# Cross-attention with layer norm: another order of all engines' work from the third tile on

## The chip, the cores and the metric

The kernel runs on one core of one Trainium2 chip. The metric is the device time of one execution in microseconds (us), the median over the runs. The engines are TensorE (PE in the profile, PEld for its weight loads), VectorE (DVE), ScalarE (ACT), GpSimd (POOL) and SyncE (SP), which issues most DMAs.

## The reference

```python
qs = (q @ wq).reshape(Bq, Lq, H, HD).transpose(0, 2, 1, 3)      # q is x: (4, 2048, 512); 16 heads of 32
ks_ = (k @ wk).reshape(Bq, Lk, H, HD).transpose(0, 2, 1, 3)     # k and v are the context: (4, 77, 512)
vs = (v @ wv).reshape(Bq, Lk, H, HD).transpose(0, 2, 1, 3)
scores = jnp.einsum('bhqd,bhkd->bhqk', qs, ks_) / jnp.sqrt(jnp.float32(HD))
scores = jnp.where(mask[:, None, :, :], -jnp.inf, scores)
attn_w = jax.nn.softmax(scores, axis=-1)
attn = jnp.einsum('bhqk,bhkd->bhqd', attn_w, vs)
out = attn.transpose(0, 2, 1, 3).reshape(Bq, Lq, H * HD) @ wo + q
mu = jnp.mean(out, axis=-1, keepdims=True)
var = jnp.mean((out - mu) ** 2, axis=-1, keepdims=True)
return (out - mu) / jnp.sqrt(var + EPS) * gamma + beta
```

All in float32. The kernel keeps the precision of the two projections with three products of a high and a low part of each operand (hi x hi, hi x lo, lo x hi).

## The kernel before, in words

The 8192 rows of x are 64 tiles of 128 rows; two tiles make a block (0 to 31) and four a group. Keys and values are made once at the start. Then every tile goes through the same steps, and the steps of many tiles are interleaved. **The order is written out by hand**, in a table of words, `ORDER` (lines 49 to 142): a letter for the step, a number for the tile, block or group, and sometimes a part. The loop at lines 732 to 744 reads it word by word and issues each step's instructions; each engine then runs its own instructions strictly in that order. The words that matter here:

- `Q` (line 275, TensorE): one quarter of a group's queries, 12 matmuls; `q` (289, VectorE) copies it out of its bank. `g`, `i`, `j` load the group's transposed x (262, SyncE), make its high part (265, ScalarE) and its low part (269, GpSimd).
- `S` (405, TensorE): the scores of a tile, 64 small matmuls into four banks. `T` (422, VectorE): mask and row maxima, four heads per word, one bank each; four words make a tile. `e` (437, ScalarE): four exponentials with their sums. `r` (447, VectorE): reciprocals of the sums; `n` (452, GpSimd): normalise; `t` (473, VectorE): transpose into B, one B per block.
- `P` (484): one of the twelve DMAs by which a block's B becomes PT, issued by the engine of its last letter: `s` SyncE, `a` ScalarE, `g` GpSimd. The words with `a` and `g` begin with block 23 and block 25.
- `V` (498, TensorE): the block's 32 matmuls with the values, into two banks; `a` (527, ScalarE) and `b` (531, VectorE): their high and low parts AH and AL.
- `O` (554, TensorE): the output product of a tile, 12 matmuls in one bank; `+` (563, VectorE) adds x, which `x` (539, SyncE) loads; `s` (577, 578, VectorE) and `v` (583 to 586, GpSimd) are the statistics; `k` (592, ScalarE), `f` (595, GpSimd) and `)` (598, GpSimd) are scale, gain and shift; `w` (601, SyncE) stores the tile. The last eight tiles use other steps for the norm.

`SLOTS` (lines 146 to 171) gives each tile buffer its place, in the order in which the table asks for them; `mm` are the eight PSUM banks. A step that takes a bank waits until the bank's last reader is done. Three buffers `pbuf` hold a tile between its maxima and its transpose, so that `T` of a tile waits for `t` of the tile three earlier.

The layer below gives each DMA of SyncE and ScalarE one of eight completion semaphores (DMAHW0 to DMAHW7), and GpSimd's one of eight others. A DMA waits, on the engine that issues it, until the DMA that had its semaphore before has landed.

Of the kernel before, what the change touches and what calls it, by code (L numbers as in the profile page):

```python
# [54 lines left out]
P1.9s P1.1s q9 Z1.s P1.11s r4 Q10 q10 e6.2 e6.1 j6 e6.3 D1 S5 T5.1 T5.3 e5.3 D2 T5.0 e5.0 Q8 q8 e6.0 j7 n4 t4 Z0.s
e5.1 S7 T7.3 e7.3 r6 T7.1 e7.1 P1.3s g8 Z5.s Z4.s T5.2 e5.2 T7.2 n6 Q14 q14 Q11 q11 Z16.s x4 g9 L1 Z13.s e7.2 Q13
Z15.s T7.0 t6 S9 T9.3 T9.0 e7.0 r7 n7 V1 T9.1 a1.0 b1.0 T9.2 r5 e9.3 x3 a1.1 b1.1 t7 P3.10s P3.1s x0 P3.11s P3.5s V0
a0.0 e9.2 b0.0 P3.6s i9 n5 t5 P2.5s O2 P3.3s P3.8s P3.9s e9.0 e9.1 S8 a0.1 T8.0 e8.0 T8.1 T8.2 e8.2 e8.1 b0.1 +2 T8.3
s2 P2.0s r9 O3 +3 s3 i8 P3.0s P3.2s O0 e8.3 j9 P3.7s P3.4s S10 T10.3 +0 T10.2 T10.0 q13 v1 k3 e10.3 r8 e10.0 T10.1
P2.2s g11 P2.11s n9 Z8.s Z14.s P2.9s P2.7s P2.6s e10.1 k2 O1 +1 s0 s1 P2.10s Q15 q15 n8 t8 Q12 P2.4s q12 S11 T11.1  # L60
T11.0 T11.2 =16.8 e10.2 v0 i11 =24.8 T11.3 r10 V3 a3.1 t9 P2.3s a3.0 b3.0 x6 P2.1s S12 T12.1 P2.8s b3.1 T12.2 x7 f2 j8
Q18 e11.0 e11.2 k1 n10 P4.4s g10 O7 f3 q18 P4.11s P4.10s )3 w3 j11 P4.9s g12 P4.5s )2 P4.6s P4.2s T12.0 S13 P4.3s V2
P4.0s T12.3 t10 e12.1 +7 s7 e11.3 e12.2 e11.1 r11 O6 T13.0 f1 P4.8s a2.1 n11 P4.7s b2.1 e12.0 P4.1s T13.2 T13.1 t11
P5.7s P5.4s +6 s6 v3 Z6.s P5.1s w2 x8 P5.10s i10 e13.0 a2.0 e12.3 e13.1 e13.2 Q19 q19 P5.3s S14 T14.3 T14.2 P5.6s r12
# [5 lines left out]
O8 +8 s8 v4 T18.2 T18.3 T18.1 e17.3 e17.0 Q20 b5.0 x10 e18.3 r17 T18.0 e18.0 e18.2 q20 n16 t16 Q21 S19 T19.0 T19.3  # L70
T19.2 T19.1 q21 P7.0s P7.2s P7.3s k8 k5 a5.1 g14 j13 x11 Q23 Z10.s q23 x13 g15 n17 f5 e18.1 r18 e19.2 Q25 t17 q25 )5
k9 V6 b5.1 S20 a6.0 e19.1 b6.0 a6.1 e19.3 e19.0 O10 n18 t18 T20.2 f9 +10 b6.1 T20.1 T20.3 )9 O11 f8 P8.3s i14 j14 L2
P8.1s S21 T21.3 w5 )8 +11 T21.1 r19 n19 Z7.s P8.0s P8.10s P8.7s P8.5s w9 T21.0 s11 T20.0 P8.2s x12 P8.9s V7 k4 e20.3
T21.2 i15 j15 O13 t19 s10 S22 T22.2 +13 e20.2 a7.0 e21.0 e20.1 e20.0 r20 e21.2 v5 f4 n20 g16 b7.0 s13 P8.8s P8.11s
e22.2 O12 +12 P8.6s T22.3 P8.4s )4 Q27 a7.1 b7.1 T22.1 t20 P9.0s P9.5s q27 P9.6s P9.10s Z12.s w8 T22.0 s12 v6 P9.8s
Q24 q24 g17 e22.3 e21.1 e21.3 r21 n21 P9.3s x16 P9.4s Q26 q26 S23 T23.2 T23.1 T23.3 k10 f10 P9.11s P9.7s e22.1 e22.0
r22 )10 n22 P9.2s k13 e23.3 T23.0 t21 V8 a8.0 S24 T24.3 Q29 P9.1s e23.0 a8.1 e23.2 T24.0 e23.1 i16 T24.2 f13 )13 b8.0
b8.1 j16 O14 P9.9s t22 T24.1 x14 +14 s14 P10.7s P10.9s P10.4s k12 e24.0 e24.1 r23 S25 T25.1 T25.3 T25.2 T25.0 e24.3
i17 e25.1 e24.2 n23 O15 x15 +15 s15 k11 w4 O16 P10.5s v7 P10.8s P10.2s t23 S26 e25.0 T26.1 j17 T26.2 P10.0s x17 w13
P10.6s +16 T26.0 f11 P10.10s r24 P10.3s k14 n24 V9 a9.1 k15 f15 T26.3 e26.3 a9.0 e25.2 e25.3 e26.1 g18 P10.11s P10.1s  # L80
w10 P11.4s P11.11s x18 O17 +17 s17 P11.1s P11.2s q29 s16 t24 r25 Q28 q28 b9.0 b9.1 Q31 q31 Q30 q30 P11.10s S27 T27.2
P11.9s P11.6s P11.0s P11.5s f14 v8 x19 P11.7s P11.8s n25 )14 e26.2 e26.0 k16 r26 e27.2 n26 T27.0 T27.1 k17 f16 )16 V10
a10.0 e27.1 a10.1 f17 )15 T27.3 e27.3 t25 S28 P11.3s g19 T28.3 T28.2 b10.1 t26 T28.1 P12.0s P12.5s O19 P12.9s P12.2s
P12.6s e28.3 O18 +18 s18 w16 +19 b10.0 Q33 q33 w14 )17 )11 w15 e27.0 r27 T28.0 n27 i19 j19 i18 e28.1 S29 T29.1 e29.1
P12.7s e28.0 V11 T29.3 T29.0 P12.10s P12.11s x21 x20 P12.1s t27 P13.5s P13.10s P12.4s g20 O21 P12.8s P13.8s O20 a11.0
T29.2 b11.0 s19 P13.2s v9 =32.8 a11.1 b11.1 e28.2 r28 n28 j18 e29.0 k18 f18 )18 S30 T30.1 e30.1 +20 T30.0 e30.0 k19
f19 T30.3 s20 +21 s21 v10 T30.2 P13.9s P12.3s x23 P13.7s P13.6s w18 P13.3s P13.0s P13.11s P13.4s w17 Q35 q35 e30.3
e29.2 P13.1s =40.8 e29.3 t28 w11 r29 n29 Q32 q32 S31 T31.2 T31.1 T31.3 O23 T31.0 e30.2 r30 n30 e31.1 Q34 q34 V12 e31.3
a12.0 t29 P14.5s L3 P14.7s f12 k21 f21 P14.2s x22 S32 T32.3 i20 g21 T32.2 b12.0 P14.9s a12.1 P14.1s P14.10s x24 )19
# [5 lines left out]
e36.2 r34 T36.1 +27 b14.1 T36.3 P16.0s O26 n34 t34 x29 f23 f22 )23 e35.2 k24 f24 P16.1s S37 T37.3 T37.2 T37.1 w12
e36.1 e35.3 T36.0 r35 n35 x28 P16.8s P16.9s w23 Q43 )24 )22 +26 P16.6s e36.3 P16.5s e37.1 a14.0 P16.3s P16.10s P16.2s
P16.4s P16.7s s27 x31 T37.0 P16.11s b14.0 Q40 V15 q40 s26 t35 P17.8s P17.2s e36.0 e37.3 v13 i22 q43 j22 P17.7s P17.3s
P17.10s P17.1s a15.0 b15.0 r36 n36 e37.2 k25 a15.1 e37.0 f25 S38 T38.2 e38.2 P17.11s )25 k26 P17.0s T38.1 O28 k27
T38.0 b15.1 +28 e38.1 r37 T38.3 e38.0 s28 Q42 q42 P17.9s w22 g24 P17.5s O29 +29 s29 w24 t36 Q41 q41 e38.3 S39 T39.1
e39.1 T39.3 e39.3 r38 T39.0 V16 a16.1 n37 t37 T39.2 S40 T40.2 T40.0 T40.1 v14 f26 k28 P17.4s P17.6s g25 T40.3 O31  # L100
b16.1 +31 e39.0 x32 s31 x30 a16.0 b16.0 P18.2s P18.1s P18.8s n38 t38 k29 e39.2 r39 O30 +30 S41 T41.2 T41.1 s30 f28 )28
Q47 q47 w28 P18.5s P18.4s Q45 P18.7s T41.3 T41.0 f27 i24 x33 )26 j24 n39 v15 t39 P18.3s e40.3 e40.2 e40.1 i25 f29 )27
w25 e41.2 e41.1 e41.0 P18.10s S42 T42.3 T42.1 T42.0 V17 k31 e40.0 T42.2 )29 a17.1 r40 n40 b17.1 k30 e41.3 e42.2
P18.11s q45 P18.0s O32 +32 P18.9s P18.6s O33 =48.8 +33 s33 a17.0 S43 e42.1 V18 a18.1 a18.0 e42.3 t40 r41 s32 g27
P19.0s P19.1s T43.3 T43.2 w27 f31 j25 n41 T43.0 T43.1 x35 P19.3s P19.5s e43.0 Q46 P19.10s w29 q46 f30 v16 P19.4s
P19.8s w26 P19.7s t41 P19.2s x34 b17.0 e42.0 r42 n42 e43.3 )30 Q44 q44 Q50 g26 P19.6s P19.9s x39 S44 T44.3 P19.11s )31
i27 j27 b18.0 T44.1 T44.2 q50 e43.2 e43.1 r43 n43 P20.6s Q48 b18.1 P20.1s t42 w31 P20.2s e44.1 i26 j26 k33 f33 )33 k32
e44.3 S45 T45.1 q48 T45.0 e45.0 T44.0 O34 O35 P20.10s +34 s34 T45.2 t43 P20.5s =56.8 Q51 V19 f32 P20.0s x36 P20.4s +35
# [692 lines left out]
```

## Time and profile before

| | us |
|---|---|
| median of three runs | 510.7 (510.17 to 511.24) |
| the profiled execution's own time | 511.24 |
| its span, first to last instruction | 509.4 |
| busy: PE, DVE, ACT, POOL | 500.0, 460.0, 474.0, 420.9 |
| mean granted TensorE clock | 0.996 |

A page shows one execution on the chip. Times in the timeline are from the span's start. An instruction counts as busy while it runs; matmuls are pipelined and their ends are modelled, so that short waits of TensorE can hide in its busy time. Where an engine was idle, the row has the time in brackets, and the last releaser that the profile finds. SPq, ACTq and POOLq are the engines' queues, where DMAs are issued; an issue is no busy time.

### The profile page before, as it was taken

To read this page: it belongs to the slowest core of one execution; us is meant where nothing else is said; L and a number is where in the kernel's file an instruction comes from. 1 tells how busy PE (TensorE), PEld (TensorE's weight loads), DVE (VectorE), ACT (ScalarE), POOL (GpSimd) and SP (SyncE) were. 2 spreads that over 40 slices of the span, in tenths; PEclk is the share of its full clock that TensorE was granted. 3 is DMA by queue.
4 is the path that set the end of the run, shared out by engine and by line. 5 is a ranking of instruction groups with operands and counts; after the bars stand their busy time and mean duration, and the time that the engine had idled before them with its cause. 6 is when DMAs were issued, how large, how long until landed. Compare 5 with 4: busy or idle time off the path is not lost.

```text
span 509.4 us, 20326 instructions
## 1 busy us (share of the span) xinstructions
PE 500.0 (98%) x6831; PEld 383.1 (75%) x6831; DVE 460.0 (90%) x2539; ACT 474.0 (93%) x2248; POOL 420.9 (83%) x387
## 2 busy tenths in 40 slices
PE   8999999999999999999999999999999999999995
PEld 6987778777777777777777777777787677867773
DVE  5799989988999998988998998899898989899997
ACT  6699999999999999999999999999997999899851
POOL 3665655978899789978898988899997999989995
PEclk9999999999999999999999999999999999999998
DMA  8957757889788978577986897868679659887745
GB/s 305 396 215 175 164 157 203 215 212 241 185 264 243 230 190 230 157 205 187 252 241 206 199 246 234 236 167 237 196 206 262 190 171 260 231 210 215 189 156 226
DMA packets 58782, 110.86 MB, mean 218 GB/s; under 512 B 9462, under 2 KB 11278, under 8 KB 58678
## 3 DMA queue, kind: packets, MB, share of 16 engines
q1 hardware_dynamic: 54502, 101.30, 70.7%
q0 software_dynamic: 2496, 5.77, 4.2%
q10 hardware_dynamic: 1680, 2.49, 1.8%
q8 instruction: 54, 0.88, 0.8%
q14 instruction: 50, 0.41, 0.3%
HBM read 41.79 MB, written 16.78 MB: 115 GB/s over the span
## 4 chain that ended last, share of the span: by engine, by line
PE 80%; DMA 5%; DVE 5%; SPq 4%; ACT 2%; POOL 2%; issue 1%; ACTq 0%; DVEq 0%; POOLq 0%
PE pq L275 29%; PE po L554 29%; PE pa L498 9%; PE sc L405 9%; DMA out<-o 2%; SPq L484 2%; DMA PT<-B 2%; DVE B L473 2%; PE pv L326 2%; PE pk L299 1%; ACT pbuf L437 1%; SPq L539 1%; DVE pbuf L422 1%; PE pq L685 1%; DMA xtf<-xT 1%
## 5 line engine op out<-in xcount | busy, mean ns | idle before, releaser
L437 ACT ACTIVATE pbuf<-pbuf,nm 128x77 f32<-128x77 f32 x1024 | 352.9, 353 | 8.4 <-DVE q L289 3.4
L437 ACT ACTIVATION_READ_ACCUMULATOR pbuf<-pbuf,nm 128x1 f32 x1024 | 197.9, 193 | 0.0
L422 DVE CUSTOM_DVE_ANT_0 pbuf<-sc,mb 128x77 f32<-128x77 f32 x1024 | 170.4, 232 | 13.4 <-PE sc L405 11.2
L452 POOL TENSOR_TENSOR pbuf<-pbuf,ri 128x1232 f32<-128x1232 f32 x63 | 142.0, 2258 | 34.6 <-DVE ri L447 28.2
L554 PE MATMUL po<-woh,AH 128*128 128x512 f32 x256 | 104.6, 409 | 0.2 <-DVE AL L531 0.2
L275 PE MATMUL pq<-xth,wqh 128*128 128x512 f32 (+1 forms) x256 | 99.9, 390 | 0.2
L554 PE MATMUL po<-woh,AL 128*128 128x512 f32 x256 | 100.0, 391 | 0.0
L554 PE MATMUL po<-wol,AH 128*128 128x512 f32 x256 | 100.0, 390 | 0.0
L473 DVE STREAM_TRANSPOSE B<-pbuf 128x1280 f32<-128x1280 f32 x64 | 95.8, 1500 | 3.4 <-DMA out<-o 0.9
L275 PE MATMUL pq<-xtl,wqh 128*128 128x512 f32 (+1 forms) x256 | 98.1, 383 | 0.0
L275 PE MATMUL pq<-xth,wql 128*128 128x512 f32 (+1 forms) x256 | 98.1, 383 | 0.0
L422 DVE DVE_READ_ACCUMULATOR2_ANT nm<- 128x1 f32 x1024 | 84.6, 83 | 0.0
L595 POOL TENSOR_TENSOR o<-o,gam 128x512 f32<-128x512 f32 x56 | 72.1, 1292 | 3.9 <-ACT o L592 3.8
L598 POOL TENSOR_TENSOR o<-o,bet 128x512 f32<-128x512 f32 x56 | 71.9, 1291 | 1.6
L269 POOL TENSOR_TENSOR xtl<-xtf,xth 128x1024 fp32r<-128x1024 f32 x28 | 67.2, 2401 | 4.8 <-ACT xth L265 4.0
L405 PEld LDWEIGHTS sc<-kct,q 32*64 32x64 f32 x4096 | 51.9, 130 | 24.9 <-issue 12.6
L405 PE MATMUL sc<-kct,q 32*64 32x77 f32 x4096 | 62.2, 238 | 1.5 <-DVE nm L422 0.9
L554 PEld LDWEIGHTS po<-woh,AH 128*128 128x128 f32 x256 | 48.0, 187 | 16.4 <-issue 3.5
L498 PE MATMUL pa<-PT,vsb 96*32 96x256 f32 x992 | 59.7, 382 | 0.0
L275 PEld LDWEIGHTS pq<-xth,wqh 128*128 128x128 f32 x256 | 48.1, 188 | 11.4 <-issue 0.8
L554 PEld LDWEIGHTS po<-woh,AL 128*128 128x128 f32 x256 | 48.1, 188 | 10.9 <-DVE AL L531 0.4
L275 PEld LDWEIGHTS pq<-xth,wql 128*128 128x128 f32 x256 | 48.1, 188 | 9.6
(108 smaller groups left out, 638.2 us busy)
## 6 DMA issues: line engine op xcount, KB each, us to landing
PT<-B SPq DMA_DIRECT2D x330, 128.0 KB
xtf<-xT SPq DMA_DIRECT2D x28, 512.0 KB
o<-x SPq DMA_DIRECT2D x56, 256.0 KB
out<-o SPq DMA_DIRECT2D x56, 256.0 KB
PT<-B POOLq DMA_DIRECT2D x25, 128.0 KB, 4.7
PT<-B ACTq DMA_DIRECT2D x17, 128.0 KB
stage_a<-kin SPq DMA_DIRECT2D x4, 410.0 KB
xtf<-xT SPq DMA_DIRECT2D x4, 256.0 KB
```

The lines of the kernel that those rows point to most:

```text
L269: return nc.gpsimd.tensor_tensor(l[:, c : c + 2], fx.pop((g, c)), xh[g][:, c : c + 2].bitcast(F32), ALU.subtract)
L275: nc.tensor.matmul(pq, w[:, c, m * P : (m + 1) * P], r[g][:, c, rs], start=(n == 0), stop=(n == 11))
L326: nc.tensor.matmul(pv[: rows.stop - rows.start], ctx_s[c][i][:, rows], v[c], start=(n == 0), stop=(n == 11))
L405: mm = nc.tensor.matmul(sc[j][r0 : r0 + SR, g * NK : (g + 1) * NK], qs[q, g, rs.start + r0 : rs.start + r0 + SR], kct[q, g, t // TPB, keys ...
L422: nc.vector.tensor_tensor_reduce(pb[:, h // 2, (h % 2) * NK : (h % 2 + 1) * NK], scs[t][j][:, g * NK : (g + 1) * NK], mb[:, t % TPB, keys_ ...
L437: nc.scalar.activation(pb[:, h // 2, (h % 2) * NK : (h % 2 + 1) * NK], pb[:, h // 2, (h % 2) * NK : (h % 2 + 1) * NK], AF.Exp, bias=nmax[t ...
L452: return nc.gpsimd.tensor_tensor(pv, pv, rv.to_broadcast((P, NP, 2, NK)), ALU.mult)
L473: nc.vector.transpose(bt.rearrange("p c q r -> p q c r"), pbuf[t % NPB].rearrange("p q (c r) -> p q c r", c=5),)
L498: nc.tensor.matmul(pas[b, g // 2][HD * j : HD * (j + 1), (g % 2) * BLK : (g % 2 + 1) * BLK], vsb[:, 2 * b // TPB, h % 2, HD * (h // 2) : H ...
L554: nc.tensor.matmul(pos[t], a[:, c, rs], w[:, c, :], start=(first and c == 0 and n == 0), stop=(c == NC_D - 1 and n == 2),)
L595: return nc.gpsimd.tensor_tensor(od[t], od[t], gam, ALU.mult)
L598: return nc.gpsimd.tensor_tensor(od[t], od[t], bet, ALU.add)
```

## The change

The table `ORDER` holds the same 2,138 words in another order; the first 60 are the same, up to the first words of the third tile. `SLOTS` follows, since buffers are asked for in another order. No step, mask or statistic is changed, and each word stays on its engine. TensorE's row is nearly the same sequence of visits: now and then a `Q` and an `O`, or an `S` and a `V`, change places. Cut to four lines of the table, and the places:

```diff
 ORDER = """
...
-e14.1 S16 T16.2 e14.3 r14 a4.1 b4.1 O9 T16.1 T15.3 P6.3s T16.0 P6.1s T16.3 e15.0 n14 t14 w7 e15.1 P6.9s S17 P6.5s
...
-e52.2 P24.8s V23 a23.0 n51 q59 t51 w40 P24.0s P24.4s P24.6s S53 O45 a23.1 )41 w41 v21 w38 e52.0 k42 P25.7a e52.3 T53.0
...
+i13 e15.3 e16.3 e16.1 P6.8s r15 n15 e16.2 S17 T17.2 g14 P6.6s V5 a5.0 a5.1 e17.2 T17.1 T17.0 T17.3 x9 P6.5s s4 t15
...
++42 w39 P24.4s S53 T53.0 s42 v21 T53.3 e53.0 P24.3a x44 i30 V23 a23.0 j30 P24.5s t51 P25.6s P25.4s w35 P24.8s T53.2
...
 SLOTS = {
     "mm": (
-        "5012367450123456702315467023616312047536420762403712056301425672015467154206701253467021534062571347"
...
+        "5012367450123456702315467023614372546310642574032165070153462705627345064723517024635120462314507614"
...
-    "xtf": "010101100101010101101010101010",
+    "xtf": "010101010101010110101010101010",
-    "o": "765401234567146204172036574036751430267521403657143201756423057",
+    "o": "765401234567215640520163527645132045173620154730264705316407215",
-    "nm": "0120120120120120120120120120120120120120120120120120120120120120",
+    "nm": "0120120121021021021021021021021021021021021021021021021021021021",
-    "ri": "0120120120120120120120120120120120120120120120120120120120120120",
+    "ri": "0120120120102102102102102102102102102102102102102102102102102102",
-    "mv": "0120120120120120120120120120",
+    "mv": "0120120120120102102102102102",
-    "rn": "0120121012012012012012012012",
+    "rn": "0120121020120120120120120120",
 }
```

In the removed lines tile 17's scores `S17` and `S53` are seen, in the added ones the same tiles: `S17`, `V5` and (in the next line) `S18` now follow each other, where `Q22` stood between `V5` and `S18`; `S53` now stands ahead of `V23` and `Q59`, where it stood behind them.

Three places in the engines' rows. The names have a running number for each buffer (PT_23 and B_23 are of block 23, sum_50 of tile 50, AH_22 of block 22). First ScalarE, where it issues its first DMAs (L484), before the change, with the semaphores that each row waits for:

```order
L437 ACTIVATE pbuf2_82,sum_50_6976<-pbuf2_82,nm_50_6936 128x77 [waits DVE_49] x7
L484 DMA PT_23_6835<-B_23_6692 32x2x512 [waits DMAHW4_49,DMAHW5_49,DMAHW3_49,DMAHW6_49,DMAHW2_49,DMAHW7_49,DMAHW1_49,DMAHW0_49]
L484 DMA PT_23_6835<-B_23_6692 32x2x512 [waits DMAHW1_49]
L437 ACTIVATE pbuf2_82,sum_50_6976<-pbuf2_82,nm_50_6936 128x77 [waits DVE_49] x4
L484 DMA PT_23_6835<-B_23_6692 32x2x512 [waits DMAHW2_49]
L592 ACTIVATE o_40_6689<-o_40_6689,rn_20_6971 128x512 [waits Pool_49]
L437 ACTIVATE pbuf2_82,sum_50_6976<-pbuf2_82,nm_50_6936 128x77 [waits DVE_49] x4
L592 ACTIVATE o_41_6525<-o_41_6525,rn_20_6971 128x512 [waits DMAHW4_49]
```

and now:

```order
L437 ACTIVATE pbuf0_80,sum_48_6643<-pbuf0_80,nm_48_6601 128x77 x4
L484 DMA PT_23_6818<-B_23_6721 32x2x512 [waits DMAHW4_49,DMAHW3_49,DMAHW5_49,DMAHW1_49,DMAHW6_49,DMAHW0_49,DMAHW7_49,DVE_49,PE_49]
L527 CAST AH_21_6820<-pa_21_1_6791 128x512 [waits Activation_49]
L592 ACTIVATE o_38_6107<-o_38_6107,rn_19_6716 128x512
L484 DMA PT_23_6818<-B_23_6721 32x2x512 [waits DMAHW2_49]
L437 ACTIVATE pbuf1_81,sum_49_6840<-pbuf1_81,nm_49_6826 128x77 [waits DVE_49] x4
L437 ACTIVATE pbuf1_81,sum_49_6840<-pbuf1_81,nm_49_6826 128x77 x4
L437 ACTIVATE pbuf1_81,sum_49_6840<-pbuf1_81,nm_49_6826 128x77 [waits DVE_49] x8
L527 CAST AH_21_6820<-pa_21_0_6790 128x512
L437 ACTIVATE pbuf2_82,sum_50_6948<-pbuf2_82,nm_50_6939 128x77 [waits DVE_49,Activation_49]
L437 ACTIVATE pbuf2_82,sum_50_6948<-pbuf2_82,nm_50_6939 128x77 [waits DVE_49] x11
L437 ACTIVATE pbuf2_82,sum_50_6948<-pbuf2_82,nm_50_6939 128x77 x4
```

The first two of these DMAs stood behind half of the exponentials of tile 50; now they stand ahead of all those of tile 49, and the third (not in these rows) behind AH of block 22. Before, the three take the semaphores DMAHW0, DMAHW1 and DMAHW2; now the two take DMAHW7 and DMAHW2.

Second SyncE, whose DMAs hold those semaphores just before. Before the change the last holders of DMAHW0 and DMAHW1 ahead of ScalarE's first two are the last two of these rows:

```order
L484 DMA PT_23_6835<-B_23_6692 32x2x512 [waits DMAHW1_49,DVE_49,PE_49]
L484 DMA PT_23_6835<-B_23_6692 32x2x512 [waits DMAHW2_49]
L484 DMA PT_23_6835<-B_23_6692 32x2x512 [waits DMAHW3_49]
L484 DMA PT_22_6652<-B_22_6421 32x2x512 [waits DMAHW4_49]
L539 DMA o_42_6934<-x 128x512 [waits DMAHW5_49]
L484 DMA PT_23_6835<-B_23_6692 32x2x512 [waits DMAHW6_49]
L601 DMA out<-o_33_5699 128x512 [waits DMAHW7_49]
L484 DMA PT_23_6835<-B_23_6692 32x2x512 [waits DMAHW0_49]
L539 DMA o_43_6966<-x 128x512 [waits DMAHW1_49]
```

and now the last holders of DMAHW7 and DMAHW2 are the second and the fifth of these; rows up to the ninth stand ahead of ScalarE's first DMA, with the last two behind it:

```order
L484 DMA PT_22_6660<-B_22_6433 32x2x512 [waits DMAHW6_49]
L484 DMA PT_22_6660<-B_22_6433 32x2x512 [waits DMAHW7_49]
L484 DMA PT_22_6660<-B_22_6433 32x2x512 [waits DMAHW0_49]
L484 DMA PT_22_6660<-B_22_6433 32x2x512 [waits DMAHW1_49]
L539 DMA o_41_6808<-x 128x512 [waits DMAHW2_49]
L484 DMA PT_22_6660<-B_22_6433 32x2x512 [waits DMAHW3_49]
L601 DMA out<-o_37_6125 128x512 [waits DMAHW4_49,Pool_49]
L484 DMA PT_22_6660<-B_22_6433 32x2x512 [waits DMAHW5_49]
L484 DMA PT_22_6660<-B_22_6433 32x2x512 [waits DMAHW6_49]
L484 DMA PT_23_6818<-B_23_6721 32x2x512 [waits DMAHW0_49,DVE_49,PE_49]
L601 DMA out<-o_36_6504 128x512 [waits DMAHW1_49,Pool_49]
```

Between holder and taker there was one other DMA before; now there are seven.

Third VectorE, where it begins the row maxima of tile 53 (sc_53), before:

```order
L422 ISA nm_52_7186 128x1
L447 RECIPROCAL ri_51_7233<-sum_51_7122 128x16
L563 TENSOR_TENSOR o_42_6934<-po_42_7235,o_42_6934 128x512
L577 BN_STATS st_42_7254<-o_42_6934 128x6
L578 BN_AGGR mv_21_7217<-st_42_7254 128x2
L531 TENSOR_TENSOR AL_22_7135<-pa_22_1_7101,AH_22_7118 128x512
L473 STREAM_TRANSPOSE B_25_7272<-pbuf2_82 128x8x5x32
L289 COPY q_14_7302<-pq_14_3_7257 128x512
L473 STREAM_TRANSPOSE B_25_7272<-pbuf0_80 128x8x5x32
L422 ISA pbuf2_82,nm_53_7378<-sc_53_0_7309,mb_3_5869 128x77
```

and now:

```order
L473 STREAM_TRANSPOSE B_25_7232<-pbuf2_82 128x8x5x32
L531 TENSOR_TENSOR AL_22_7203<-pa_22_1_7109,AH_22_7126 128x512
L447 RECIPROCAL ri_51_7261<-sum_51_7092 128x16
L577 BN_STATS st_43_7265<-o_43_6937 128x6
L578 BN_AGGR mv_21_7267<-st_43_7265 128x2
L563 TENSOR_TENSOR o_42_6993<-po_42_7248,o_42_6993 128x512
L422 ISA pbuf2_82,nm_53_7308<-sc_53_0_7272,mb_3_6050 128x77
L422 ISA nm_53_7308 128x1
```

The two transposes into B_25 are those of tiles 50 (from pbuf2) and 51 (from pbuf0). Both stood ahead of the first maxima of tile 53; now the second stands behind half of them, ahead of the other half.

More of the change, by code (lines that the diff above doesn't have):

```diff
@@ L55 @@
[L55 to L64, printed above, removed]
@@ L70 @@
[L70 to L79, printed above, removed]
@@ L80 @@
[L80 to L89, printed above, removed]
@@ L95 @@
[L95 to L104, printed above, removed]
@@ L105 @@
[L105 to L108, printed above, removed]
-s35 v17 P20.9s P20.7s P20.3s x37 P20.8s e44.2 T45.3 e44.0 r44 n44 P20.11s )32 g29 P21.9s w30 e45.2 e45.3 S46 T46.2 q51
@@ new lines @@
+v16 t41 e43.3 V18 a18.0 a18.1 Q46 Q50 )31 =48.8 e43.1 e43.0 q46 q45 P20.5s i27 j27 P20.3s S44 P20.1s P20.9s x38 w27
+q50 b18.0 P20.10s P20.7s T44.1 T44.0 x37 w31 T44.2 t42 O34 k33 T44.3 f33 e43.2 i26 k32 e44.0 e44.1 S45 T45.0 r43
+P20.2s P20.6s T45.1 e45.1 P20.4s e44.2 T45.3 e45.3 +34 s34 Q48 O35 b18.1 q48 +35 s35 T45.2 e44.3 j26 r44 n43 t43 )30
+f32 v17 n44 e45.2 )33 k35 P20.11s w30 Q51 V19 e45.0 P20.0s k34 a19.1 S46 T46.3 T46.2 T46.0 e46.0 P20.8s P21.9s e46.2
+e46.3 )32 T46.1 e46.1 Q49 b19.1 f34 )34 r45 t44 f35 )35 S47 T47.1 T47.0 e47.1 =56.8 P21.0s n45 q49 O36 x36 g29 i29
@@ L142 @@
+y62 O63 s63 )53 w53 z62 w62 u63 y63 z63 w63
 """
```

135 lines of the change are left out of this document (87 added, 48 removed).

## The prediction

> **What bounds the kernel now.** I read the page first, then the busy time by stage, the chain of waits, and last the timeline of single engines where the stages showed idle time. The page's first part:
>
> ```profile
> PE 500.0 (98%) x6831; PEld 383.1 (75%) x6831; DVE 460.0 (90%) x2539; ACT 474.0 (93%) x2248; POOL 420.9 (83%) x387
> ```
>
> The table by stage (us; for each engine its busy time and instructions, then the granted clock, the DMA share and GB/s):
>
> ```profile
> 60.00:384.00 324.00, 324.00 (x4511) 247.41 (x4516) 296.96 (x1721) 318.71 (x1529) 277.83 (x230) 1.00 0.78 213
> 384.00:408.00 24.00, 22.70 (x381) 16.75 (x377) 20.96 (x141) 22.81 (x105) 20.69 (x17) 1.00 0.79 224
> 408.00:496.00 88.00, 87.53 (x1128) 65.84 (x1131) 82.17 (x395) 78.38 (x380) 80.95 (x98) 1.00 0.76 205
> 496.00:510.00 14.00, 7.28 (x46) 4.98 (x38) 9.79 (x17) 3.06 (x8) 8.05 (x13) 0.84 0.56 214
> ```
>
> TensorE has no idle time from 60 to 384 us. It loses 1.30 us in the 24 us behind that, 0.47 us in the next 88, and the rest at the end. So the span is TensorE's work plus a start and an end, and a new order can only win what TensorE waits in the middle. What that work costs stands in the chain of waits, which keeps to TensorE there (start, us, what):
>
> ```profile
> 100.00 0.88 PE sc L405 x52
> 100.88 1.86 PE pa L498 x32
> 102.74 2.96 PE po L554 x12
> 105.70 2.72 PE pq L275 x12
> ```
>
> A projection or an output product of 12 matmuls takes 2.72 us, one tile's scores 0.88, one block's product with the values 1.86; the first 12 matmuls behind such small tiles take 0.24 more (2.96). The new order has the same visits, so this sum stays but for those 0.24.
>
> Now the middle. The scores of tile 54, TensorE's timeline:
>
> ```profile
> 402.05 0.34 PE L405 MATMUL sc<-kct,q 32*64 32x77 f32 x2
> 402.89 0.31 PE L405 MATMUL sc<-kct,q 32*64 32x77 f32 x2 [0.49 <-DVE nm L422]
> 403.40 0.34 PE L405 MATMUL sc<-kct,q 32*64 32x77 f32 x2 [0.20 <-DVE AL L531]
> 404.12 0.89 PE L405 MATMUL sc<-kct,q 32*64 32x77 f32 x58 [0.38 <-DVE nm L422]
> 404.94 0.50 PE L554 MATMUL po<-woh,AH 128*128 128x512 f32 x1
> ```
>
> From 402.05 to 404.94 are 2.89 us where 0.88 are work: 2.01 us of waiting, most of it modelled as busy. The banks are held by VectorE's row maxima of tile 53. One more wait, at the output product of tile 42, costs 0.23:
>
> ```profile
> 390.71 0.50 PE L554 MATMUL po<-woh,AH 128*128 128x512 f32 x1 [0.23 <-DVE AL L531]
> ```
>
> Why is VectorE late? Its timeline ahead of this:
>
> ```profile
> 386.71 1.51 DVE L473 STREAM_TRANSPOSE B<-pbuf 128x1280 f32<-128x1280 f32 x1
> 389.96 0.69 DVE L531 TENSOR_TENSOR AL<-pa,AH 128x512 fp32r<-128x512 f32 x1 [1.74 <-ACT AH L527]
> ...
> 400.64 1.49 DVE L473 STREAM_TRANSPOSE B<-pbuf 128x1280 f32<-128x1280 f32 x1
> 402.06 0.20 DVE L422 CUSTOM_DVE_ANT_0 pbuf<-sc,mb 128x77 f32<-128x77 f32 x1
> ...
> 402.66 0.69 DVE L531 TENSOR_TENSOR AL<-pa,AH 128x512 fp32r<-128x512 f32 x1
> 403.26 0.23 DVE L422 CUSTOM_DVE_ANT_0 pbuf<-sc,mb 128x77 f32<-128x77 f32 x1
> ```
>
> It stood idle for 1.74 us, waiting for ScalarE's high half of block 22. And ScalarE was late for this reason:
>
> ```profile
> 380.32 0.36 ACT L437 ACTIVATE pbuf<-pbuf,nm 128x77 f32<-128x77 f32 x1 [0.34 <-DVE nm L422]
> 380.68 0.35 ACT L437 ACTIVATE pbuf<-pbuf,nm 128x77 f32<-128x77 f32 x1
> ...
> 381.36 0.34 ACT L437 ACTIVATE pbuf<-pbuf,nm 128x77 f32<-128x77 f32 x1
> ...
> 382.88 2.27 ACTq L484 DMA_DIRECT2D PT<-B  x2
> 385.19 0.36 ACT L437 ACTIVATE pbuf<-pbuf,nm 128x77 f32<-128x77 f32 x1 [3.40 <-DVE q L289]
> ```
>
> ScalarE was idle for 3.40 us between two exponentials, and in that gap its queue issued its first two DMAs of regrouped weights. The releaser named, a VectorE copy of the queries, writes nothing that this exponential reads (pbuf and nm), so it was another. The program's rows shown above have the reason: the two DMAs use semaphores DMAHW0 and DMAHW1, whose holders just before them are two issues of SyncE:
>
> ```profile
> 379.74 0.59 SPq L484 DMA_DIRECT2D PT<-B  x1
> 380.38 0.59 SPq L539 DMA_DIRECT2D o<-x  x1
> ```
>
> ScalarE's first DMA could only go once the one of 379.74 had landed (3.14 us later, at 382.88); its second, which ends the row at 385.15 after 0.59 of issuing, once the one of 380.38 had, some 4.2 us on. All work queued behind on ScalarE waited with them.
>
> **The change, part by part.** *The ScalarE wait.* In the new order the first two such DMAs stand 24 exponentials (24 x 0.35 = 8.4 us) earlier in ScalarE's row, and take semaphores whose holders were issued eight DMAs ahead, not two; the third, with a holder six ahead, stands behind the high half of block 22. Price of the wait: 3.40 us on ScalarE, 1.74 on VectorE, 2.01 + 0.23 = 2.24 us on TensorE, which nothing hides, because TensorE is never idle behind it. Bounds: none of it goes (0), or all of it, and with it the 0.47 of the next stage (2.71). I take 2.24, since the program's rows show no near holder left there.
>
> *What is late next.* In the new order VectorE has the transpose of tile 51 between the maxima of tile 53, so the scores of tile 54 wait for GpSimd's normalise of tile 51, then 1.5 us of transpose and two groups of four maxima, 0.60 each (402.06 to 402.66). GpSimd's rows:
>
> ```profile
> L452 POOL TENSOR_TENSOR pbuf<-pbuf,ri 128x1232 f32<-128x1232 f32 x63 | 142.0, 2258 | 34.6 <-DVE ri L447 28.2
> L595 POOL TENSOR_TENSOR o<-o,gam 128x512 f32<-128x512 f32 x56 | 72.1, 1292 | 3.9 <-ACT o L592 3.8
> L598 POOL TENSOR_TENSOR o<-o,bet 128x512 f32<-128x512 f32 x56 | 71.9, 1291 | 1.6
> L269 POOL TENSOR_TENSOR xtl<-xtf,xth 128x1024 fp32r<-128x1024 f32 x28 | 67.2, 2401 | 4.8 <-ACT xth L265 4.0
> ```
>
> From the gain of tile 40 (which waits for ScalarE's scale) to the end of that normalise the new order has two gains, two shifts, two normalises and one split: 4 x 1.29 + 2 x 2.26 + 2.40 = 12.1 us, the same as before from there. If ScalarE is 3.4 us earlier, GpSimd's previous normalise becomes the start, some 1.2 us earlier than now: the scores then come with 0 to 0.6 us of waiting. I take 0.3.
>
> *Fewer changes of tile form.* The score and value blocks are followed by full-size matmuls 58 times before, 57 now (tile 17's scores, value block 5, tile 18's scores stand together): 0.24 us less, on the path.
>
> *That same place, as a cost.* Tile 18's scores now come 1.86 us behind tile 17's and need two groups of maxima, 1.2 us, of tile 17 done. VectorE must start on them within 0.6 us. The old order has seven such places, and at the five in front of 380 us TensorE shows no idle time. Between 0 and about 1 us (a queued transpose of 1.5 us less that slack); I take 0.1.
>
> *All else.* Behind the third tile nearly every instruction has other neighbours, with the same work per engine. TensorE has no idle time there up to 384 us, so this part can only cost: nothing, or some 0.5 at each place like the 0.49 in the row above. I take 0.2: one such place, less a chance that the 0.47 of the stage behind 408 us shrinks.
>
> Sum: -2.24 + 0.3 - 0.24 + 0.1 + 0.2 = -1.88 us, about -1.9. Against its own execution: span 509.4 to 507.5, with the 1.84 around it (511.24 less 509.4) 509.3. That execution was the slowest of three; the median lies 0.54 lower, so 510.7 - 1.9 = **508.8 us**.
>
> **The rivals.** A measurement of this kernel can tell about 0.2%, 1.0 us, from no change.
>
> *The ScalarE wait comes back elsewhere (no change).* One of ScalarE's new DMAs, the one for piece 9 of block 24, takes the semaphore that the store of tile 40 had three DMAs ahead. That store needs GpSimd's gain and shift of tile 40, behind ScalarE's scale: a round trip of 1.29 + 1.29, 0.59 of issue and a landing. For 256 KB the load of 380.38 above gives about 4.2 from its issue, so 6.8 in all. ScalarE meanwhile has one scale, 16 exponentials, two halves and a cast:
>
> ```profile
> L592 ACT ACTIVATE o<-o,rn 128x512 f32<-128x512 f32 x56 | 44.8, 812 | 1.0 <-POOL rn L586 0.9
> L527 ACT CAST AH<-pa 128x512 fp32r<-128x512 f32 x64 | 35.9, 574 | 5.6 <-PE pa L498 4.5 <-PE pa L513 1.2
> L265 ACT CAST xth<-xtf 128x1024 fp32r<-128x1024 f32 x28 | 29.0, 1039 | 0.4 <-PE pq L275 0.4
> ```
>
> With exponentials 0.35 apart that is 0.81 + 16 x 0.35 + 2 x 0.57 + 1.04 = 8.6 us, so 1.8 to spare; a normalise (2.26) in front on GpSimd turns this into a wait of 0.5. If GpSimd or SyncE is 3 us later still, the old 3.4 us are back and with them TensorE's 2.24: -1.88 + 2.24 = +0.4, so 511.1; half of it gives 510.0. For it: a store is a late holder. Against: the slack. The Trainium skill (SBUF — State Buffer, "The DMA setup-cost knee") puts a transfer at 2 us plus its bytes at 436 GB/s: 2.6 us for these 256 KB, an estimate from that page. By it the round trip would be about 1.6 us shorter and this rival nearly out; the load above took 4.2, and the measurement decides.
>
> *GpSimd becomes the late one (slower).* The place is again tile 54's scores, but through the transpose of tile 51. GpSimd's normalises of tiles 50 and 51 in the old order:
>
> ```profile
> 394.93 4.47 POOL L452 TENSOR_TENSOR pbuf<-pbuf,ri 128x1232 f32<-128x1232 f32 x2
> ```
>
> The second ends at 399.4. In the new order the scores are due at 402.05 less 0.23 and 0.24, about 401.6, and can come 1.5 + 1.2 = 2.7 us behind the end of that normalise; each us by which it ends later than 398.9 is a us on TensorE. The point that decides is 402.1: then the wait is 3.2 us and the sum -1.88 - 0.3 + 3.2 = +1.0. With a normalise and a shift more in front (2.26 + 1.29 = 3.5, so 402.9) it is 4.0, or +1.8: 512.5. For it: GpSimd is busy for 20.69 of this stage's 24 us, and here all that it has is in one row. Against: its work up to there is the same as before, and ScalarE, which starts it, comes earlier.
>
> **How the numbers follow.** The forecast, with its own range from 507.8 (all waits of the middle gone and no new one: -2.9) to 509.7, has a chance of 0.62; the first rival, 509.7 to 511.7, 0.22; the second, above 511.7, 0.16. The range for 8 in 10 reaches from 507.4 (below -2.9 by the spread of the runs around their median, about 0.4) to 512.2, into the second rival. Faster by over 0.2% is the forecast's case (0.62), within 0.2% the first rival's (0.22), slower the second's (0.16).
>
> **What would show it.** Right: no idle time near 3.4 us on ScalarE around its first DMAs of regrouped weights; TensorE's 24 us behind 384 nearly full; the scores of tile 54 in about 1 us; the last matmul about 2 us earlier and the end behind it as long as now. Wrong: ScalarE idle in front of a DMA issue at L484 (first rival); VectorE idle at L473 on GpSimd, and TensorE with it (second); or TensorE idle between 60 and 384 us, where it has none now, which would say that the change of order costs in places that I have not priced.

## The result and the profile after

The changed kernel takes 507.65 us (median of 20 runs, 507.09 to 510.31), the kernel before 510.59 (median of 20 runs, 508.76 to 515.35): ratio 0.9944, 95% interval 0.9928 to 0.996. That is 2.9 us less; the forecast was 1.9 less (508.8). The profiled execution of the changed kernel took 507.98 with a span of 506.2, against 511.24 and 509.4. Its engines did the same work:

```profile
PE 498.8 (99%) x6831; PEld 383.1 (76%) x6831; DVE 460.5 (91%) x2539; ACT 473.9 (94%) x2248; POOL 421.3 (83%) x387
```

The stages, with the columns as before:

```profile
60.00:384.00 324.00, 323.99 (x4499) 247.64 (x4497) 297.66 (x1728) 321.63 (x1550) 277.74 (x231) 1.00 0.80 217
384.00:408.00 24.00, 24.00 (x392) 18.25 (x392) 22.81 (x142) 23.45 (x111) 22.87 (x17) 1.00 0.76 216
408.00:496.00 88.00, 88.00 (x1140) 66.12 (x1139) 83.58 (x397) 78.37 (x367) 81.44 (x100) 1.00 0.77 212
```

TensorE is full from 60 to 496 us. The 1.30 us that it lost between 384 and 408 and the 0.47 behind that are gone. The place that carried the prediction, tile 54's scores on TensorE, was four rows over 2.89 us and is now one:

```profile
401.84 0.95 PE L405 MATMUL sc<-kct,q 32*64 32x77 f32 x64
```

ScalarE now issues its first two DMAs of regrouped weights here:

```profile
370.64 0.72 ACTq L484 DMA_DIRECT2D PT<-B  x1
371.40 0.59 ACT L527 CAST AH<-pa 128x512 fp32r<-128x512 f32 x1 [0.41 <-ACT pbuf L437]
371.45 0.69 ACTq L484 DMA_DIRECT2D PT<-B  x1
```

The idle time around them is 0.41 us, where it was 3.40. The last matmul ends at 500.04 us (503.28 before), and the end behind it is as long as it was, 6.2 us.

### The profile page after: what moved, and what is told of

It reads as the page before. It is cut to its first block, busy times and chain, and to the rows that moved or that the text cites. A ratio compares the mean times of both kernels' runs of the same rounds, so it can differ in the third digit from the quotient of the medians.

```text
span 506.2 us, 20312 instructions
## 1 busy us (share of the span) xinstructions
PE 498.8 (99%) x6831; PEld 383.1 (76%) x6831; DVE 460.5 (91%) x2539; ACT 473.9 (94%) x2248; POOL 421.3 (83%) x387
## 4 chain that ended last, share of the span: by engine, by line
PE 98%; DMA 1%; DVE 1%; ACT 0%; issue 0%; DVEq 0%
PE po L554 36%; PE pq L275 35%; PE pa L498 11%; PE sc L405 11%; PE pv L326 2%; PE pk L299 1%; PE pq L685 1%; DMA stage_a<-kin 1%; PE pa L513 0%; DVE xtl L637 0%; PE po L543 0%; DVE st L606 0%; DVE po L634 0%; ACT woh L672 0%; DVE mvt L608 0%
## 5 line engine op out<-in xcount | busy, mean ns | idle before, releaser
L437 ACT ACTIVATION_READ_ACCUMULATOR pbuf<-pbuf,nm 128x1 f32 x1024 | 203.2, 198 | 0.0
L554 PE MATMUL po<-woh,AH 128*128 128x512 f32 x256 | 103.5, 404 | 0.0
```

The costliest lines, as they stand in the source:

```text
L437: nc.scalar.activation(pb[:, h // 2, (h % 2) * NK : (h % 2 + 1) * NK], pb[:, h // 2, (h % 2) * NK : (h % 2 + 1) * NK], AF.Exp, bias=nmax[t ...
L554: nc.tensor.matmul(pos[t], a[:, c, rs], w[:, c, :], start=(first and c == 0 and n == 0), stop=(c == NC_D - 1 and n == 2),)
```

## The experiments

Two theories stood against each other. **Theory 1:** what the kernel before loses late is ScalarE waiting, at its own DMA issues, for other DMAs to land. **Theory 2:** it is the order of the late rows, above all VectorE's, whatever ScalarE does. In the new order both are changed at once. Each median and ratio is against runs of the kernel before beside it on the same chip: 509.70 us beside the first four kernels below, 509.9 beside the first repeat, the changed kernel's repeat, the five DMAs and the late normalise, 510.74 beside the crossings at tile 46.

**Only ScalarE's first three DMAs set back, in the kernel before.** They stand behind exponentials that were queued behind them (the third behind four of these and two scales), and keep their semaphores:

```diff
-P23.11a T50.1 P23.0a t48 e50.1 Q52 q52 ... w39 P23.4s P23.5a k40 f40 )40 )38 e50.2 k41
+T50.1 t48 e50.1 P23.11a Q52 q52 ... w39 P23.4s k40 f40 )40 )38 e50.2 P23.0a k41 P23.5a
```

> The kernel before, with ScalarE's first three DMAs of regrouped weights (block 23, pieces 11, 0 and 5) set 4, 8 and 8 exponentials further back in ScalarE's row; they keep the semaphores and the holders that they had, and nothing else moves. Theory 1 (the loss comes from ScalarE's wait at these DMAs): the 3.40 us gap goes, with it 2.01 us at tile 54's scores and 0.39 at tile 42's output product, and the later 0.29 and 0.46 at tiles 56 and 60 at most in part; 2.4 to 3.0 us faster than before, about 508. Theory 2 (the loss comes from how the late stage's rows are ordered, above all VectorE's): ScalarE's gap goes, but tile 54's scores still wait about 2 us; no change within 0.5 us.

Measured 508.84 us; ratio 0.9988, interval 0.9972 to 1.0004, so by time alone no more than a hint. Its profile (508.69) shows the mechanism. ScalarE around the DMAs, then tile 54's scores:

```profile
381.91 0.71 ACTq L484 DMA_DIRECT2D PT<-B  x1
383.40 0.81 ACT L592 ACTIVATE o<-o,rn 128x512 f32<-128x512 f32 x1 [0.17 <-POOL rn L586]
384.12 0.61 ACTq L484 DMA_DIRECT2D PT<-B  x1
384.81 0.59 ACTq L484 DMA_DIRECT2D PT<-B  x1
```

```profile
401.58 0.95 PE L405 MATMUL sc<-kct,q 32*64 32x77 f32 x64
```

With ScalarE's gap gone the old late order has no wait at tile 54. That is theory 1, at this place. Why the median moved by only 0.9 us and not 2.4, the repeats of the kernel before show, further down.

**The wait put back into the changed kernel.** Its first two DMAs are moved behind tile 50's first exponentials:

```diff
-... e48.3 P23.5a a21.1 b20.1 ... n48 w36 P23.11a T49.1 ... T50.0 e50.0 P23.3s T50.3 e50.3 ...
+... e48.3 a21.1 b20.1 ... n48 w36 T49.1 ... T50.0 e50.0 P23.5a P23.11a P23.3s T50.3 e50.3 ...
```

> The changed kernel, with ScalarE's first two DMAs of regrouped weights (block 23, pieces 5 and 11) moved behind the first exponentials of tile 50, where the kernel before had its first two; their semaphores are then last held by SyncE's piece 9 and by its load of tile 42's x (issued at 377.4 and 378.0 in the changed kernel's trace), so that ScalarE waits there for about 2 us. Theory 1: tile 51's reciprocals, normalise and transpose come about 1.4 us later, and tile 54's scores 1.0 to 1.4 us; 508.7 to 509.1. Theory 2: the new rows take the wait up; within 0.4 us of the changed kernel, 507.7 to 508.1.

Measured 513.41 us, ratio 1.0082 (1.0054 to 1.011). I had the wait too short: the first DMA went 7.4 us after the issue of SyncE's piece 9 (375.84), and ScalarE stood idle for 6.07 us, not 2. The trace keeps the time at which each of the sixteen parts of a DMA landed: those of piece 9 did between 380.80 and 383.20, and ScalarE's DMA went at 383.22. What spread them out, it does not show.

```profile
383.22 1.61 ACTq L484 DMA_DIRECT2D PT<-B  x2
384.88 0.36 ACT L437 ACTIVATE pbuf<-pbuf,nm 128x77 f32<-128x77 f32 x1 [6.07 <-DVE nm L422]
```

TensorE's waits are back at three places: 1.65 at the output product of tile 42, then here (tile 45's product and tile 54's scores):

```profile
401.05 0.47 PE L554 MATMUL po<-woh,AH 128*128 128x512 f32 x1 [0.59 <-DVE nm L422]
403.99 0.35 PE L405 MATMUL sc<-kct,q 32*64 32x77 f32 x4
405.05 0.34 PE L405 MATMUL sc<-kct,q 32*64 32x77 f32 x2 [0.71 <-DVE nm L422]
405.69 0.90 PE L405 MATMUL sc<-kct,q 32*64 32x77 f32 x58 [0.29 <-DVE nm L422]
```

The new rows do not take the wait up: against theory 2.

**Both crossings.** One kernel is the old one up to 383.9 us, ScalarE's three DMAs included, and the new late order from there; the other is the new one up to 384 us and the old late order. Tile and bank slots behind the seam were dealt out anew. The words at the two seams:

```diff
-... k41 f41 P23.9s P23.7s x45 V22 a22.0 g30 e51.2 i31 j31 t49 P24.10a ...
+... k41 f41 P23.9s P23.7s x45 w37 g30 P23.3s T51.3 e51.3 r50 n50 V22 a22.0 a22.1 i31 j31 t49 ...
```

```diff
-... P23.8s P23.7s Q55 q55 S51 T51.3 e51.3 T51.1 T51.2 r50 n50 V22 a22.0 a22.1 P23.0a i31 j31 t49 ...
+... P23.8s P23.7s Q55 q55 S51 w35 P23.0a T51.1 T51.0 T51.2 w39 f41 V22 a22.0 e51.2 i31 j31 t49 ...
```

> The kernel before up to the product of block 22 with the values (383.9 us), ScalarE's first three DMAs and their wait with it, and from there the rest in the changed kernel's order. Theory 1: ScalarE waits 3 to 4 us at 382 us, and the changed kernel's late stage pays for it: tile 54's scores 1.5 to 2.5 us late, 509.5 to 510.5 in all. Theory 2: the new late order alone brings the gain, about 508.

Measured 511.91 us, ratio 1.0057 (1.0037 to 1.0077): slower than before. ScalarE and TensorE in it (its line numbers are six lower, its table being printed in fewer lines):

```profile
382.99 1.38 ACTq L478 DMA_DIRECT2D PT<-B  x2
384.42 0.36 ACT L431 ACTIVATE pbuf<-pbuf,nm 128x77 f32<-128x77 f32 x1 [2.88 <-DVE q L283]
```

```profile
387.31 0.89 PE L399 MATMUL sc<-kct,q 32*64 32x77 f32 x58 [0.62 <-DVE nm L416]
...
402.28 0.35 PE L399 MATMUL sc<-kct,q 32*64 32x77 f32 x4
403.22 0.34 PE L399 MATMUL sc<-kct,q 32*64 32x77 f32 x2 [0.59 <-DVE nm L416]
403.85 0.90 PE L399 MATMUL sc<-kct,q 32*64 32x77 f32 x58 [0.29 <-DVE nm L416]
```

With a gap of 2.88 us the new late order loses 1.51 us at tile 54 (2.01 in the old one) and 0.92 at tile 52's scores. From the start of tile 52's scores to that of tile 56's it takes 32.94 us, against 32.72 in the kernel before and 29.97 in the changed one. Theory 2 falls here: the new late order alone brings nothing.

> The changed kernel up to the scores of tile 51 (384 us), with ScalarE's first two DMAs early and no wait, and from there the rest in the order of before. Theory 1: no wait of 3.4 us on ScalarE, so tile 54's scores come without the 2.01 us, and the small waits of before at tiles 56 and 60 (0.29 and 0.46) stay; 508.0 to 508.7. Theory 2: the old late order brings its 2 us back; about 510.3.

Measured 509.59 us, ratio 1.0001 (0.9989 to 1.0014), where I expected 508.0 to 508.7. Tile 54's scores still take 1.24 us too long. The first two DMAs do not wait, but the third, piece 0 of block 23, does:

```profile
386.59 0.61 ACTq L478 DMA_DIRECT2D PT<-B  x1
387.30 0.59 ACT L521 CAST AH<-pa 128x512 fp32r<-128x512 f32 x1 [2.42 <-PE sc L399]
```

ScalarE was idle from 384.88 and had nothing in its row ahead of this DMA. The piece of SyncE that held its semaphore was issued at 378.30, and its last part landed at 386.57, 0.02 us before the issue. The releaser named in the row, the scores, is not what it waited for. The old late order has this DMA ahead of block 22's high half, and the new one behind it. So the seam brought a wait of theory 1's kind with it: this run does not speak for theory 2, and it cannot show the old late order without such a wait.

**The kernel before again, three times.** No edit; the question was why the first experiment's median moved so little.

> The kernel before, unchanged, for a second profile of it. Theory 1 says that the cost is a wait for DMAs to land, which need not take the same time in each execution: in this profile ScalarE's gap at its first DMAs and tile 54's wait move together, and an execution of 509.7 (the median beside the first four experiments) has a smaller gap than the 3.40 us of the profile of 511.24: 2.2 to 2.8 us of gap, 0.8 to 1.5 us of wait at tile 54. Theory 2 (the order of the rows): a wait of about 2 us at tile 54 whatever the gap is.

> The kernel before once more, one look for a third pair of ScalarE's gap at its first DMAs (3.40 and 2.82 us so far) and tile 54's wait (2.01 and 1.85). Theory 1: they move together, and an execution of about 509.5 has a gap under 2.5 us and a wait of 0.5 to 1.3 us. Theory 2: the wait stays near 2 us.

> The kernel before once more, for a fourth pair of ScalarE's gap and tile 54's wait. Theory 1: they move together, a gap under 2.5 us with a wait of 0.5 to 1.3 us. Theory 2: the wait stays near 2 us.

These three profiles are of executions of 513.83, 511.41 and 510.08 us (the first with a median of 510.32, ratio 1.0007, 0.9977 to 1.0036; the other two single looks). ScalarE in the last of them, the fourth profile of before:

```profile
382.23 1.63 ACTq L484 DMA_DIRECT2D PT<-B  x2
383.91 0.36 ACT L437 ACTIVATE pbuf<-pbuf,nm 128x77 f32<-128x77 f32 x1 [1.82 <-DVE nm L422]
```

The gap is 1.82 us here, 2.71 and 2.23 in the other two, 3.40 in the profile that I predicted from. The load that holds the second semaphore was issued at 379.96 to 380.51 in the four, and the DMA that waits for it went 3.22 to 4.17 us later: the same program waits for another landing time in each execution.

That ScalarE waits for these landings is not only inferred from the program's rows. The last part of the first holder landed at 382.86, 382.70, 382.66 and 382.21 in the four profiles, and ScalarE's first DMA went 0.02 us later each time (at 382.88, 382.72, 382.68 and 382.23). For the second DMA the landing came 0.02 to 0.03 us ahead. Of the gap, 1.3 us are the two issues themselves (1.9 in the third profile, where the second issue took 1.20). The rest is nearly all waiting for the landings: 2.1 us in the first profile and 0.5 in the fourth.

Tile 54's wait alone is 2.01, 1.85, 1.37 and 0.96 us in the four. It falls with the gap, as theory 1 has it, though it is longer for a given gap than was expected; none of the three executions was as fast as the 509.5 to 509.7 asked for. (The 2.82 in the second text is 2.71 in the row.) The tile's wait is not the whole price, since part of the loss in the first profile falls ahead of tile 53. What TensorE pays is read from the starts of tile 52's and tile 56's scores, in the first profile of before and in the changed kernel:

```profile
386.59 0.95 PE L405 MATMUL sc<-kct,q 32*64 32x77 f32 x64
...
419.31 0.95 PE L405 MATMUL sc<-kct,q 32*64 32x77 f32 x64 [0.22 <-DVE q L289]
```

```profile
386.87 0.95 PE L405 MATMUL sc<-kct,q 32*64 32x77 f32 x64
...
416.84 0.95 PE L405 MATMUL sc<-kct,q 32*64 32x77 f32 x64
```

That is 32.72 us before and 29.97 after, for the same visits. All profiles, in us (the last matmul's end closes the last stretch):

| kernel | ScalarE's gap at its first DMAs | tile 52 to 56 | tile 56 to 60 | tile 60 to the end |
|---|---|---|---|---|
| before, first profile | 3.40 | 32.72 | 29.80 | 54.17 |
| before, second | 2.71 | 32.04 | 31.42 | 55.84 |
| before, third | 2.23 | 31.55 | 30.45 | 54.16 |
| before, fourth | 1.82 | 31.13 | 29.96 | 54.18 |
| three DMAs set back | 0.17 | 29.95 | 29.95 | 54.21 |
| five DMAs set back | none | 29.96 | 29.69 | 53.63 |
| changed, first profile | none | 29.97 | 29.65 | 53.54 |
| changed, second | none | 29.90 | 29.65 | 53.43 |

In the four executions of the kernel before, the stretch less the gap is 29.32, 29.33, 29.32 and 29.31: each us of ScalarE's gap beyond some 0.6 is a us on TensorE. This is theory 1 with its price. It also says why one profile misled: the first had the longest of four gaps. The mean stretch of the four is 31.86, so these four lose 1.9 us here on average, not 2.75. Three of them are of executions slower than the median, and the first experiment's median gained only 0.9 us, so an execution at the median loses less, about 1 us by that.

**Two more of ScalarE's DMAs.** The table has a second loss, behind tile 56. In the profile of the first experiment ScalarE still stood idle for 1.88 us at a DMA of block 27 (1.97 in the text below). Here two DMAs of that block are set back too:

```diff
-P27.7a P27.1g ... v24 e58.3 t56 x50 S59 T59.3 T59.0 a25.0 P27.4a b25.0 Q62 q62 e58.0 P27.9s ...
+P27.1g ... v24 e58.3 P27.7a t56 x50 S59 T59.3 T59.0 a25.0 b25.0 Q62 q62 e58.0 P27.4a P27.9s ...
```

> The kernel before with five of ScalarE's DMAs set back in its row: the three of the first such experiment, and two of block 27 (pieces 7 and 4) behind the next four exponentials; semaphores and holders as before. In the first experiment's profile ScalarE still waited 1.97 us at piece 7 of block 27, and TensorE 0.30 and 0.46 us at tile 60's scores. Theory 1 (each of these losses is a wait of ScalarE at a DMA): the 1.97 us go and with them most of the 0.76; 506.2 to 506.5 of span, so the same time as the changed kernel within 0.4 us. Theory 2: the 0.76 stay, since VectorE's copy of the last quarter of group 15's queries sets them; 506.9 of span again.

Measured 508.69 us, ratio 0.9973 (0.9947 to 0.9999), span 506.5. First ScalarE and tile 60's scores in the third profile of before, then in this kernel:

```profile
441.17 0.61 ACTq L484 DMA_DIRECT2D PT<-B  x1
441.83 0.36 ACT L437 ACTIVATE pbuf<-pbuf,nm 128x77 f32<-128x77 f32 x1 [2.37 <-DMA out<-o]
```

```profile
449.31 0.39 PE L405 MATMUL sc<-kct,q 32*64 32x77 f32 x16 [0.71 <-DVE q L289]
449.90 0.82 PE L405 MATMUL sc<-kct,q 32*64 32x77 f32 x48 [0.20 <-DVE q L289]
```

```profile
438.99 0.61 ACTq L484 DMA_DIRECT2D PT<-B  x1
439.64 0.59 ACT L527 CAST AH<-pa 128x512 fp32r<-128x512 f32 x1 [0.63 <-DMA out<-o]
```

```profile
446.69 0.95 PE L405 MATMUL sc<-kct,q 32*64 32x77 f32 x64
```

The gap shrinks from 2.37 to 0.63 and tile 60's scores run through. Here too the landing decides, and not the store that the rows name: in the third profile of before the last part of the load of tile 52's x, which held the semaphore of this DMA, landed at 441.00, 0.17 us ahead of the issue. TensorE waited there for VectorE's copy of the last quarter of the queries, as theory 2 had it, but VectorE was late because ScalarE was: the two theories name the last two links of one chain. From tile 52 to the last matmul this kernel takes 113.28 us, the changed one 113.16 and 112.98.

**The changed kernel beside these.**

> The changed kernel, unchanged, beside the others on one chip: 507.0 to 507.7, with a ratio to before of 0.994 to 0.997; no gap on ScalarE at its first DMAs, no wait at tile 54's scores.

Measured 507.75 us, ratio 0.9949 (0.9925 to 0.9972), 0.05 above the expected range. That is 0.9 us below the five DMAs set back, where at most 0.4 was expected. Two more crossings, with the seam at tile 46's scores (about 345 us), far ahead of ScalarE's DMAs, ask where that comes from:

```diff
-... )32 g29 P21.9s w30 e45.2 e45.3 S46 T46.2 q51 T46.0 T46.3 P21.5s g28 ...
+... )32 g29 P21.9s w30 e45.2 e45.3 S46 x38 e45.1 k35 k34 a19.1 T46.3 T46.2 T46.0 e46.0 ...
```

```diff
-... Q51 V19 e45.0 P20.0s k34 a19.1 S46 T46.3 T46.2 T46.0 e46.0 P20.8s P21.9s ...
+... Q51 V19 e45.0 P20.0s k34 a19.1 S46 x39 =56.8 x36 P20.8s )32 g29 P21.9s T46.2 q51 ...
```

> The kernel before up to the scores of tile 46 (about 345 us), then the rest in the changed kernel's order, ScalarE's DMAs of regrouped weights included, with the semaphores that they have there. Question: where does the last 1 us between the kernel before with five DMAs set back (508.69) and the changed kernel (507.75) come from? If from the first 345 us (one change of tile form, 0.24 us, and short waits such as one of 0.58 us at tile 18's scores): 508.0 to 508.4. If from the late stage: 507.5 to 507.8, the changed kernel's time.

> The other way round: the changed kernel up to the scores of tile 46, then the order of before with the five DMAs set back. If the last 1 us comes from the first 345 us: 507.7 to 508.1. If from the late stage: 508.4 to 508.7.

The first, with the old order for 345 us and the new one behind, took 508.03 us, ratio 0.9952 (0.9936 to 0.9967): the whole gain within its interval. The second took 509.08, ratio 0.9973 (0.9953 to 0.9993): that of the five DMAs set back. The first time lies at the edge of the answer "from the first 345 us" and the second in neither range, but the kernel before was 0.8 us slower beside these two (510.74), so that the ratios count. By them 345 us of another order move nothing that can be told here, and what was left lies late; the two intervals overlap a little. The profiles agree: from tile 52's scores to the last matmul the first takes 113.08 us and the second 114.47. In the second one's profile ScalarE's gap at block 27 is back at 2.17 us with the DMAs set back, and tile 60's scores wait 0.59 and 0.20: in that profile setting them back by four exponentials did not cover the landing, in the other it nearly did. That this makes up the last 0.9 us is likely from these two profiles, not shown.

**GpSimd's normalise of tile 51 made late**, in the changed kernel:

```diff
-... O42 r51 n51 P24.7s s43 +42 w39 P24.4s S53 T53.0 s42 v21 T53.3 ...
+... O42 r51 P24.7s s43 +42 w39 P24.4s S53 T53.0 s42 v21 n51 T53.3 ...
```

> The changed kernel with GpSimd's normalise of tile 51 moved behind the four small operations of block 21's norm (which wait for VectorE's moments of tile 42). In the changed kernel's trace that normalise ends at 398.0; here it should end at about 402.1, the point at which the second rival of the prediction decides. By its chain (transpose 1.5, two groups of maxima 1.2) tile 54's scores then come at about 405.0, 3.2 us late: 510.7 to 511.2. If the chain has slack that the prediction did not see, less than 2 us.

Measured 512.19 us, ratio 1.003 (1.0006 to 1.0053), 4.4 us above the changed kernel. The normalise and tile 54's scores:

```profile
403.25 2.26 POOL L452 TENSOR_TENSOR pbuf<-pbuf,ri 128x1232 f32<-128x1232 f32 x1
```

```profile
405.32 0.35 PE L405 MATMUL sc<-kct,q 32*64 32x77 f32 x4
407.71 0.34 PE L405 MATMUL sc<-kct,q 32*64 32x77 f32 x2 [2.04 <-DVE nm L422]
408.35 0.90 PE L405 MATMUL sc<-kct,q 32*64 32x77 f32 x58 [0.29 <-DVE nm L422]
```

It ends 15.15 us behind the start of tile 52's scores (390.36 here), 3.1 us beyond the 12.0 that the prediction's chain allows (398.9 less the changed kernel's 386.87); the stretch from tile 52 to 56 is 32.91, 2.97 longer than without. The chain and its price hold. The other 1.4 us of the median are not in this place; the last section has what goes with them.

## Why the prediction was right

Forecast -1.9 us in a range of 507.4 to 512.2; measured -2.9 and 507.65. The range held it; the forecast's own range (507.8 to 509.7) ended 0.15 too high. By its steps:

*The ScalarE wait (-2.24).* The mechanism was right, and is shown from both sides: taking the gap from the old kernel removes the wait at tile 54, putting one into the new kernel brings it back, and over four executions the loss follows the gap us for us. The landings that the trace keeps come just ahead of the issues and leave no other cause for the gap. The size is -2.75 in the execution that the sum was made from, which includes the small waits at tile 42's output product and tile 56's scores, -1.9 in the mean of four, and -0.9 by the first experiment's median (its interval reaches from -1.4 to +0.2). So the sum came out near for the wrong size: 2.24 is too much for an execution at the median, and what that left open was made up elsewhere.

*What is late next (+0.3).* Nothing. GpSimd's normalise of tile 51 ended at 398.0, ahead of the 398.9 from which it would cost, and VectorE, which began its transpose at 398.72, went through the transpose into the maxima without a pause:

```profile
395.71 2.27 POOL L452 TENSOR_TENSOR pbuf<-pbuf,ri 128x1232 f32<-128x1232 f32 x1
```

*Fewer changes of tile form (-0.24), tile 18's scores (+0.1).* Tile 17's scores, value block 5 and tile 18's scores follow each other without a wait:

```profile
130.36 0.95 PE L405 MATMUL sc<-kct,q 32*64 32x77 f32 x64
131.24 1.93 PE L498 MATMUL pa<-PT,vsb 96*32 96x256 f32 x32
133.10 0.99 PE L405 MATMUL sc<-kct,q 32*64 32x77 f32 x64
```

So the second term is 0. The first cannot be told apart: from the eighth quarter of the queries (30 us) to tile 46's scores the four profiles of before take 314.58 to 315.26 us, the two of the changed kernel 314.49 and 314.30, and executions of one order differ by 0.7.

*All else (+0.2).* This is the step that failed: "this part can only cost". It brought most of the rest. In the means of the profiles that is 1.4 us from tile 56's scores on: 0.76 up to tile 60 (30.41 against 29.65, nearly half of it from the second profile, of an execution of 513.83) and 0.68 behind it (54.17 against 53.49, without that profile). The 0.68 goes with block 27's wait as well: where it stayed, the last stretch is 54.21 (three DMAs set back), and where it shrank, 53.63 (five). With the 1.9 above, the means give 3.3 us for a measured 2.9, since three of the four profiles are of executions slower than the median; how the 2.9 of the medians divide is not shown closer. The old profile had the cause in plain sight, a gap of 1.31 us on ScalarE at 443.48 with a store named as its releaser, at its DMA of block 27. I counted TensorE's 0.47 of that stage into a bound and did not follow it back, as I had done at tile 54; it is the same wait at a second place, and in other executions it is longer (2.35 and 0.87, 2.37, 1.79).

*First rival (the wait comes back at block 24's piece 9).* It did not. The store that holds the semaphore, and then ScalarE's DMA behind an exponential:

```profile
388.60 0.95 SPq L601 DMA_DIRECT2D out<-o  x2
```

```profile
391.46 0.35 ACT L437 ACTIVATE pbuf<-pbuf,nm 128x77 f32<-128x77 f32 x1
391.58 0.59 ACTq L484 DMA_DIRECT2D PT<-B  x1
```

The DMA went 2.98 us behind the store's issue without any idle time. The store's last part had landed at 391.40, only 0.18 us ahead; in the second profile of the changed kernel the margin is 0.26, and with the old order ahead of tile 46 it is 0.48. The slack of 1.8 us was not there: with the landing of 4.2 that I had put, the DMA would have waited 1.2 us. That the wait stayed away was luck. The Trainium skill (SBUF — State Buffer, "The DMA setup-cost knee") puts a transfer at 2 us plus its bytes at 436 GB/s, an estimate of 2.6 us for these 256 KB. This store took 2.80 and those of the other two profiles 2.20 and 1.99, while the loads at 380 us took 3.20 to 4.14. One figure for a landing was the mistake, from whichever source.

*Second rival (GpSimd late).* Did not occur, 0.9 us away from its threshold; the experiment with the late normalise shows that its place and price were right.

## What to carry to other kernels

A DMA issued by a computing engine is a place where that engine can stop: it waits for whichever DMA had its semaphore before, and everything queued behind waits too. Give such an issue some microseconds behind that holder in the engine's row, follow every wait of the bound engine back to such a place and not only the longest one, and take more than one profile before pricing a wait on a landing: here the same gap was 1.8 to 3.4 us in four executions. The releaser that a row names for such a gap can be wrong; the sign to look for is a DMA issue of the engine's own queue inside the gap.
